# One layer of banded attention and 4-bit dequantized linear: three changes to the order of work on VectorE and POOL

## The chip, the core and the metric

The kernel runs on one core of one Trainium2 chip. A core has TensorE (PE in the profile, with its weight loads as PEld), VectorE (DVE), ScalarE (ACT), GpSimd (POOL) and SyncE (SP, which issues most of the DMAs). Each engine works through its own queue in order; engines wait for each other through semaphores. Matmul results land in PSUM, everything else lives in SBUF. The metric is the device time of one execution in microseconds (us); lower is better.

## The reference

There are 2048 rows of 1024 values, and two stages, each with a residual and a normalization of the rows:

```python
attn = jnp.einsum('ds,td->st', w1, w2) * sparse_mask
y = jnp.einsum('bds,st->bdt', x, attn) + b2
x = _layernorm(x + jax.nn.gelu(y, approximate=False), axis=-1)

e = jnp.linalg.norm(x, axis=-1)
y_l = jnp.einsum('bsi,oi->bso', x, dequant_kbit(qweight, lut4, 4))
y_h = jnp.einsum('bsi,oi->bso', x, dequant_kbit(qweight, lut8, 8))
x = _layernorm(x + jnp.where((e > 64.0)[..., None], y_h, y_l) + bias, axis=-1)
```

`dequant_kbit` builds a 1024 x 1024 weight: bit p of each weight's code comes from bit plane p of `qweight`, and the code picks one of 16 (or 256) values of the output row's table. The mask is banded: it is one only near the diagonal. After the first normalization a row's norm is near 32, so the 8-bit weight is needed only where a row is odd; the kernel counts such rows, and entries of the mask outside the band, and takes a general path if there is any. With these inputs there is none.

## The kernel before

The 2048 rows are 16 tiles of 128 rows. The kernel has four stages, by the time of the profile:

- Up to about 50 us the band of `attn` is made (line 464), with `w2` transposed on TensorE.
- Tiles 0 to 15 go through `attention(n)` (lines 581 to 602). TensorE multiplies the transposed tile with the band on top of b2, which ScalarE copied into the PSUM accumulator before (`fill_b2`, line 505); ScalarE applies gelu (585); VectorE adds the residual and sums the rows (590); `stats` (383) makes the rows' mean on POOL (`nm`, 387), the sum of squares on ScalarE (`junk`, 390) and the factor `r` on POOL (392, 393); and VectorE normalizes the tile in place (`normalize`, 397), for which it needs `r`.
- Meanwhile the 4-bit weight is made in eight blocks of 128 output rows, two blocks (a pair) at a time (`dequantize_pair`, 309). `unpack` (295) spreads the bits of a pair with eight small VectorE instructions. A block has two sides. On each side, ScalarE makes three of the four table entries for bit 0 (`e`, 329) and POOL the fourth (`root`, 333), and VectorE folds them by bits 1 and 2 with three copy_predicated (336 to 338); a last one folds the two sides by bit 3 (346), and the unit matrix is added (349) so that the product carries the residual too. TensorE transposes the block (281) and ScalarE copies it to `wT` (282). The generator is advanced step by step, `steps(1)`, between the tiles, two steps per block. The blocks of a pair are numbered 0 to 7 here; pair 2 is blocks 4 and 5, pair 3 is blocks 6 and 7.
- Tiles 0 to 3 are multiplied with the left half of the weight as soon as blocks 0 to 3 are there (`ffn_half`, 645, "left"), with one attention between each two, and with the right half later; the other twelve tiles go in pairs (`ffn_pair`, 714) from about 200 us to the end. After a left or right product VectorE adds bias (`combine`, 619), which also frees the accumulator.

The order of an engine's queue is not that of the calls. A scheduler of the framework orders the instructions by its own costs and the tiles' buffers; `tc.issue_after(x)` makes every instruction issued inside it, on the engine of `x`, come after `x` in that engine's queue, and holds nothing on other engines. From tile 8 on (`("attention", 8)`, line 876) VectorE's queue is in the order of the calls. The normalization of a tile is not called with its tile: `attention` puts it into a list, and `now()` calls what is in the list, up to tile 8 after the next tile's residual has been called. That is an order of calls alone: the scheduler could put the previous tile's normalization ahead of the next tile's residual, and the unpacks wherever they fit. PSUM has two accumulators `mm` for attentions and half products and four `pt` for transposes.

Of the kernel before, what the change touches and what calls it, by code (L numbers as in the profile page):

```python
# [14 lines left out]
ALU = mybir.AluOpType  # L15
# [6 lines left out]
KT = D // P  # L22
# [170 lines left out]
def kernel(  # L193
# [13 lines left out]
    nc = tc.nc  # L207
# [7 lines left out]
    with ExitStack() as main:  # L215
# [92 lines left out]

        def dequantize_pair(pair):

            bits = bits_of[pair]
            for t in range(2):
                ot = 2 * pair + t

                def plane(p):
                    return bits[:, t * B_L + p, :]

                roots = []
                for side in range(2):
                    root = dq.tile([P, D], FP, tag="root", name="root", bufs=4)  # L320
                    roots.append(root)
                    entry = [root] + [
                        dq.tile([P, D], FP, tag="e", name="e", bufs=7) for _ in range(3)
                    ]
                    for j in (1, 2, 0, 3):
                        k = 4 * side + j
                        d_k, l_k = diff[:, ot, k : k + 1], lt[:, ot, 2 * k : 2 * k + 1]
                        if j:
                            nc.scalar.activation(  # L329
                                entry[j], plane(0), AF.Identity, scale=d_k, bias=l_k  # L330
                            )
                        else:
                            nc.gpsimd.tensor_scalar(  # L333
                                entry[j], plane(0), d_k, l_k, ALU.mult, ALU.add
                            )
                    nc.vector.copy_predicated(entry[2], plane(1), entry[3])  # L336
                    nc.vector.copy_predicated(root, plane(1), entry[1])  # L337
                    nc.vector.copy_predicated(root, plane(2), entry[2])  # L338
                    if side == 0:
                        if t == 1 and pair + 1 < KT // 2:  # L340
                            if pair == 0:
                                tc.keep_in_program_order(differences(2, KT))
                            unpack(pair + 1)
                        yield
                w_nat = roots[0]
                nc.vector.copy_predicated(w_nat, plane(3), roots[1])  # L346

                own = w_nat.rearrange("o (s b) -> o s b", s=8)[:, :, ts(ot, P // 8)]
                nc.vector.tensor_tensor(
                    own, own, ident.rearrange("o (b s) -> o s b", s=8), ALU.add  # L350
                )
                transpose_pending(1)
                pending.append((ot, w_nat))
                yield
# [57 lines left out]
        with tc.tile_pool(name="prod", bufs=1) as prod:  # L412
# [45 lines left out]
            behind = ExitStack()  # L458
# [57 lines left out]
        behind_copy = [None]  # L516
# [57 lines left out]
        def now():  # L574
            while later:
                later.pop(0)()

        def nothing():
            pass

        def attention(n, xT, meanwhile=nothing):
            xt = x_tiles[n]
            ps = band_rows(xT)
# [3 lines left out]
                now()  # L587
            meanwhile()
            total = work.tile([P, 1], FP, tag="total", name="total", bufs=4)
            nc.vector.scalar_tensor_tensor(xt, z, 1.0, xt, ALU.mult, ALU.add, accum_out=total)  # L590
            nm, r, ss = stats(xt, total)

            if n <= 2 * EARLY:
                now()

            def rest():
                normalize(xt, xt, nm, r)
# [277 lines left out]
        for i, (what, n) in enumerate(todo):  # L875
# [27 lines left out]
                    ready = prepare(*todo[i + 1])  # L903
            if (what, n) in unpack_after:

                first = behind_copy[0] if (what, n) == ("left", 0) else masked
                with tc.issue_after(first.ins):
                    steps(1)
        first_ps.close()
        ps_pair = main.enter_context(  # L910
# [54 lines left out]
```

## Time and profile before

Three runs took 357.08, 357.35 and 357.87 us, median 357.35. The profiled execution took 358.36 us, and its span from the first instruction to the last is 356.6 us.

| | busy us | share of the span | instructions |
|---|---|---|---|
| PE | 329.1 | 92% | 1227 |
| DVE | 211.2 | 59% | 310 |
| ACT | 178.7 | 50% | 257 |
| POOL | 114.7 | 32% | 162 |

The mean granted clock of TensorE is 0.978. By stretch, busy us of each engine and the granted clock:

| us | length | PE | DVE | ACT | POOL | PEclk |
|---|---|---|---|---|---|---|
| 57 to 70 | 13 | 12.28 | 11.24 | 8.77 | 10.41 | 1.00 |
| 70 to 82 | 12 | 8.38 | 6.72 | 9.69 | 7.34 | 0.72 |
| 82 to 94 | 12 | 12.00 | 8.71 | 10.52 | 0.00 | 1.00 |
| 94 to 106 | 12 | 12.00 | 10.00 | 11.85 | 5.05 | 1.00 |
| 106 to 118 | 12 | 12.00 | 10.92 | 9.70 | 6.08 | 1.00 |
| 118 to 130 | 12 | 12.00 | 9.95 | 10.70 | 8.51 | 1.00 |
| 130 to 143 | 13 | 9.33 | 8.64 | 9.54 | 2.09 | 0.87 |
| 143 to 156 | 13 | 13.00 | 4.09 | 9.62 | 4.18 | 0.99 |
| 156 to 350 | 194 | 189.92 | 99.91 | 55.22 | 50.61 | 1.00 |

In the lines of the profile, `L560` is line 560 of the kernel, `out<-in` are the program's names without buffer numbers, `x20` is a number of instructions merged into one row, and `[1.24 <-ACT mm L505]` says that the engine was idle for 1.24 us before it, and that ScalarE's instruction of line 505 ended the wait. An engine may wait for several things; the last is named. A POOL instruction's duration holds the time in which it could not reach SBUF.

### The profile page before, as it was taken

How to read it: one execution, taken by the hardware profiler on the slowest of the kernel's cores; microseconds unless marked ns; L12 is line 12 of the kernel's file. 1: busy time of each engine (PE TensorE's matmuls, PEld its weight loads, DVE VectorE, ACT ScalarE, POOL GpSimd, SP SyncE). 2: the span in 40 equal slices, each digit the busy share in tenths (PEclk: the TensorE clock that was granted, in tenths of full speed). 3: DMA queues.
4: the chain of work that ended last, by engine and by line, in shares of the span. 5: the costliest groups of instructions: out<-in, count | busy, mean ns of one | idle time of the engine just before them, and what ended most of it. 6: DMA issues, size and time to landing. Idle time of an engine off the chain costs nothing.

```text
span 356.6 us, 3693 instructions
## 1 busy us (share of the span) xinstructions
PE 329.1 (92%) x1227; PEld 203.3 (57%) x1228; DVE 211.2 (59%) x310; ACT 178.7 (50%) x257; POOL 114.7 (32%) x162
## 2 busy tenths in 40 slices
PE   6799989959999987999999998999999999999990
PEld 6587769845676576966655643444444443444450
DVE  0579898846888885336476853554635525733342
ACT  4696997488997887774346311304214115023020
POOL 1632523870326442324423630502304104004010
PEclk9999999969999998999999999999999999999997
DMA  8999219400000000320264425153554450441103
GB/s 253 317 320 383 90 60 370 160 0 0 1 2 0 0 2 0 149 90 34 72 218 165 140 81 177 59 198 101 202 186 139 181 175 22 192 141 59 59 8 121
DMA packets 28475, 43.91 MB, mean 123 GB/s; under 512 B 7584, under 2 KB 20640, under 8 KB 28448
## 3 DMA queue, kind: packets, MB, share of 16 engines
q1 hardware_dynamic: 26832, 42.66, 34.8%
q10 hardware_dynamic: 1616, 0.93, 0.9%
q8 instruction: 12, 0.20, 0.2%
q14 instruction: 15, 0.12, 0.1%
HBM read 28.90 MB, written 14.68 MB: 122 GB/s over the span
## 4 chain that ended last, share of the span: by engine, by line
PE 60%; DVE 17%; POOL 9%; ACT 5%; issue 4%; DMA 3%; POOLq 0%; DVEq 0%; ACTq 0%
PE u L724 20%; PE mm L607 10%; PE w L724 10%; PE mm L560 8%; PE v L724 6%; POOL root L333 4%; DVE e L336 4%; PE pt L281 3%; DVE root L338 3%; DVE root L346 2%; DMA w_raw<-in_L_attn_w_dram 2%; DVE root L337 2%; POOL nm L387 2%; DVE x L590 2%; PE mm L464 1%
## 5 line engine op out<-in xcount | busy, mean ns | idle before, releaser
L390 ACT ACTIVATE junk<-x,total 128x1024 bf16<-128x1024 f32 x31 | 35.6, 1150 | 64.9 <-DVE total L632 26.2
L560 PE MATMUL mm<-attn,xT 128*128 128x198 f32 (+2 forms) x320 | 62.2, 351 | 5.5 <-ACT mm L505 5.5
L560 PEld LDWEIGHTS mm<-attn,xT 128*128 128x128 f32 x320 | 54.0, 195 | 13.7 <-ACT mm L505 6.9
L329 ACT ACTIVATE e<-v,lt,diff 128x1024 f32<-128x1024 uint8 x48 | 56.9, 1247 | 6.2 <-DVE v L299 3.2
L607 PE MATMUL mm<-wT,xT 128*128 128x512 f32 x128 | 57.8, 605 | 0.0
L333 POOL TENSOR_SCALAR root<-v,diff,lt 128x1024 f32<-128x1024 uint8 x16 | 39.5, 2476 | 44.4 <-DVE root L346 23.2
L387 POOL TENSOR_SCALAR nm<-total 128x1 f32<-128x1 f32 x31 | 19.3, 624 | 77.5 <-DVE x L590 48.9
L724 PE MATMUL u<-t,halves 128*128 128x512 f32 x96 | 43.3, 593 | 1.0 <-DVE x L744 1.0
L607 PEld LDWEIGHTS mm<-wT,xT 128*128 128x128 f32 x128 | 24.4, 196 | 27.8 <-issue 27.3
L710 POOL TENSOR_TENSOR halves<-halves 128x512 f32<-128x512 f32 x6 | 9.5, 1589 | 84.0 <-DVE halves L707 67.8
L706 ACT COPY halves<-rows 128x1024 f32<-128x1024 f32 x6 | 6.3, 1042 | 55.3 <-DMA rows<-there 55.3
L464 PE MATMUL mm<-w2T,w_sb 128*128 128x268 f32 (+1 forms) x128 | 29.2, 377 | 4.2 <-ACT w2T L282 3.6
L724 PEld LDWEIGHTS u<-t,halves 128*128 128x128 f32 x96 | 18.2, 190 | 24.3 <-issue 22.2
L674 DVE STREAM_TRANSPOSE squares<-x 128x1024 f32<-128x1024 f32 x12 | 24.4, 2030 | 11.0 <-DMA there<-squares 11.0
L397 DVE TENSOR_SCALAR x<-x,nm,r 128x1024 f32<-128x1024 f32 x16 | 13.0, 812 | 28.6 <-POOL r L393 24.0
L464 PEld LDWEIGHTS mm<-w2T,w_sb 128*128 128x128 f32 x128 | 22.8, 189 | 8.1 <-ACT w2T L282 4.3
L281 PE MATMUL pt<-ident,x 128*128 128x128 f32 x160 | 22.4, 286 | 3.6 <-ACT wT L282 3.6
L590 DVE SCALAR_TENSOR_TENSOR x<-z,x 128x1024 f32<-128x1024 f32 x16 | 20.5, 1281 | 7.7 <-ACT z L585 7.7
L336 DVE COPY_PREDICATED e<-v,e 128x1024 f32<-128x1024 uint8 x16 | 22.7, 1422 | 3.3 <-ACT e L329 3.3
L281 PEld LDWEIGHTS pt<-ident,x 128*128 128x128 f32 x160 | 19.8, 155 | 6.9 <-ACT wT L282 4.2
L337 DVE COPY_PREDICATED root<-v,e 128x1024 f32<-128x1024 uint8 x16 | 21.0, 1315 | 3.9 <-POOL root L333 3.4
L724 PE MATMUL v<-wT,halves 128*128 128x512 f32 x48 | 22.7, 594 | 0.0
(93 smaller groups left out, 437.6 us busy)
## 6 DMA issues: line engine op xcount, KB each, us to landing
x<-in_L_attn_x_dram SPq DMA_DIRECT2D x16, 512.0 KB, 7.6
out_dram<-o SPq DMA_DIRECT2D x14, 512.0 KB, 2.6
there<-squares SPq DMA_DIRECT2D x12, 512.0 KB, 3.1
rows<-there SPq DMA_DIRECT2D x48, 128.0 KB, 2.9
w_raw<-in_L_attn_w_dram SPq DMA_DIRECT2D x8, 512.0 KB, 6.8
w_sb<-in_L_attn_w_dram SPq DMA_DIRECT2D x3, 1024.0 KB, 7.8
w_sb<-in_L_attn_w_dram SPq DMA_DIRECT2D x2, 512.0 KB, 7.1
x<-_L_attn_sparse_mask_dram SPq DMA_DIRECT2D x2, 413.0 KB, 3.7
```

The costliest lines, as they stand in the source:

```text
L281: nc.tensor.transpose(pt[:, j, :], block(g * (HALF // P) + j), ident)
L329: nc.scalar.activation(entry[j], plane(0), AF.Identity, scale=d_k, bias=l_k)
L333: nc.gpsimd.tensor_scalar(entry[j], plane(0), d_k, l_k, ALU.mult, ALU.add)
L336: nc.vector.copy_predicated(entry[2], plane(1), entry[3])
L337: nc.vector.copy_predicated(root, plane(1), entry[1])
L387: nc.gpsimd.tensor_scalar(nm, total, -1.0 / D, None, ALU.mult)
L390: nc.scalar.activation(junk, u, AF.Square, scale=float(-D), bias=total, accum_out=ss)
L464: part = nc.tensor.matmul(out=ps[:, : hi - lo], lhsT=w1_sb[s][:, k, :], rhs=w2T[:, k, lo:hi], start=(k == 0), stop=(k == KT - 1),)
L560: behind_mm[0] = nc.tensor.matmul(out=ps[:, a:b], lhsT=xT[:, s, :], rhs=attn[:, s, a - lo : b - lo], start=False, stop=hi == D or (h == 0 ...
L590: nc.vector.scalar_tensor_tensor(xt, z, 1.0, xt, ALU.mult, ALU.add, accum_out=total)
L607: nc.tensor.matmul(out=ps, lhsT=xT[:, k, :], rhs=wT[:, k, ts(h, HALF)], start=(k == 0), stop=(k == KT - 1),)
L724: nc.tensor.matmul(out=ps, lhsT=a[:, k, :], rhs=b[:, k, :], start=start and k == 0, stop=stop and k == KH - 1, skip_group_check=True,)
```

## The change

Three edits.

1. In `attention`, for tiles 0 to 8, the previous tile's normalization is put behind this tile's residual in VectorE's queue, by `issue_after`; it was only called after it.
2. The bits of pair 2 (blocks 4 and 5) are unpacked in the generator's first step of pair 2 itself, and no longer in the third step of pair 1. That step is the one taken after `("left", 0)`; in it, VectorE's instructions now come after the last mask multiplication and after the latest residual called, that of tile 3, and ScalarE's after the copies of the early tile, as before. (Before, in that step, nothing on VectorE was held.)
3. In blocks 4 to 7, the entry `j == 2` of the second side is made on POOL and not on ScalarE: four instructions.

In the built programs the queues of TensorE and SP are unchanged. VectorE's queue has the same instructions: the residuals of tiles 1, 2 and 3 come earlier, the normalizations of tiles 0 to 2 each come after the next tile's residual (that of tile 3 is called by the left product of tile 0 and is not bound), and all 16 unpacks of pairs 2 and 3 follow tile 3's residual, five ahead of tile 3's normalization and eleven behind it. Further on, the copies of blocks 4 to 7 stand in another order around the combines; the last block's are all ahead of the combine of tile 3's left half, where four instructions of block 7 came after it. In POOL's queue the entries of block 4 and 5 now stand behind the statistics of tiles 1 to 3, five entries in a row, and later entries stand in part between a tile's sum and its factor. ScalarE's queue has four entries less.

```diff
         def dequantize_pair(pair):
 
+            if pair == 2:
+                unpack(pair)
             bits = bits_of[pair]
...
-                        if j:
+                        if j and not (ot > 3 and side and j == 2):
                             nc.scalar.activation(
                                 entry[j], plane(0), AF.Identity, scale=d_k, bias=l_k
                             )
                         else:
                             nc.gpsimd.tensor_scalar(
                                 entry[j], plane(0), d_k, l_k, ALU.mult, ALU.add
                             )
...
-                        if t == 1 and pair + 1 < KT // 2:
+                        if t == 1 and pair + 1 < KT // 2 and pair != 1:
...
+        behind_sum = [None]
...
-            nc.vector.scalar_tensor_tensor(xt, z, 1.0, xt, ALU.mult, ALU.add, accum_out=total)
+            summed = behind_sum[0] = nc.vector.scalar_tensor_tensor(
+                xt, z, 1.0, xt, ALU.mult, ALU.add, accum_out=total
+            )
             nm, r, ss = stats(xt, total)
 
             if n <= 2 * EARLY:
-                now()
+                with tc.issue_after(summed.ins):
+                    now()
...
-                first = behind_copy[0] if (what, n) == ("left", 0) else masked
-                with tc.issue_after(first.ins):
+                with ExitStack() as behind:
+                    behind.enter_context(tc.issue_after(masked.ins))
+                    if (what, n) == ("left", 0):
+                        behind.enter_context(tc.issue_after(behind_copy[0].ins))
+                        behind.enter_context(tc.issue_after(behind_sum[0].ins))
                     steps(1)
```

## The prediction

> **What bounds the kernel now.** I read the page's slices first, then who made TensorE wait, then the order of time of each engine between 57 and 156 us. The slices say where TensorE is not full:
>
> ```profile
> PE   6799989959999987999999998999999999999990
> PEclk9999999969999998999999999999999999999997
> ```
>
> One slice is 8.9 us. After the start there are two dips, at 71 to 80 us and at 134 to 143 us, and in both the granted clock (PEclk) dips too. From 155.76 us to the last matmul TensorE waits only 0.37 and 1.00 us, so what reaches 155.76 earlier ends earlier. The waits of TensorE, in all us, times, longest:
>
> ```profile
> PE mm L560 <- ACT mm L505: 5.5, 4, 2.4
> PE pt L281 <- ACT wT L282: 3.6, 2, 2.8
> ```
>
> TensorE in order of time (start, us, line, idle before and releaser):
>
> ```profile
> 69.64 1.91 PE L281 MATMUL pt<-ident,root 128*128 128x128 f32 x16
> 74.39 2.51 PE L281 MATMUL pt<-ident,x 128*128 128x128 f32 x12 [2.84 <-ACT wT L282]
> 77.67 1.11 PE L281 MATMUL pt<-ident,x 128*128 128x128 f32 x4 [0.77 <-ACT wT L282]
> 78.58 8.59 PE L607 MATMUL mm<-wT,xT 128*128 128x512 f32 x16
> ...
> 132.40 3.86 PE L560 MATMUL mm<-attn,xT 128*128 128x198 f32 x20 [1.24 <-ACT mm L505]
> 136.10 1.04 PE L281 MATMUL pt<-ident,x 128*128 128x128 f32 x8
> 139.56 5.54 PE L560 MATMUL mm<-attn,xT 128*128 128x198 f32 x20 [2.43 <-ACT mm L505]
> ```
>
> The product at 78.58 took 8.59 us, the later ones 7.03; the attention at 139.56 took 5.54, others 3.76. So each dip costs its wait and 1.6 to 1.8 us of half clock. ScalarE is the one named, but it was itself held in its queue, by VectorE:
>
> ```profile
> 71.71 1.15 ACT L390 ACTIVATE junk<-x,total 128x1024 bf16<-128x1024 f32 x1 [4.88 <-DVE x L590]
> ...
> 131.33 1.02 ACT L505 COPY mm<-b_bc 128x1024 f32<-128x1024 f32 x1 [1.45 <-DVE x L619]
> ```
>
> And VectorE in order of time, with its largest wait between 76 and 140 us below:
>
> ```profile
> 70.46 1.21 DVE L590 SCALAR_TENSOR_TENSOR x<-z,x 128x1024 f32<-128x1024 f32 x1
> ...
> 110.86 2.04 DVE L338 COPY_PREDICATED root<-v,e 128x1024 f32<-128x1024 uint8 x1
> ...
> 130.62 0.67 DVE L619 SCALAR_TENSOR_TENSOR x<-mm,bias_bc 128x512 f32<-128x512 f32 x1
> ```
>
> ```profile
> DVE x L397 <- POOL r L393: 7.5, 4, 3.5
> ```
>
> ```profile
> 108.30 3.40 POOL L333 TENSOR_SCALAR root<-v,diff,lt 128x1024 f32<-128x1024 uint8 x1 [8.05 <-DVE root L346]
> ```
>
> The residual of tile 2 (L590 at 70.46) had its gelu at 66.84; it stood behind a normalization (L397) that waited 1.02 us for POOL's r, and behind unpacks. From 80.74 (first copy_predicated of block 4) to 135.56 VectorE is the slow one: 28 copies, and TensorE at 132 and 139 waits for what comes after them. POOL's entry at 108.30 waited for VectorE until 110.82, then ran, and VectorE's next copy took 2.04 us instead of 1.31: the two exclude each other.
>
> **The change part by part.** Lines are those of before.
>
> *Edits 1 and 2, normalizations behind the next residual, block 4 and 5 unpacked behind tile 3's residual.* Nothing is added or removed; 16 unpacks (0.20 us each) and four normalizations (0.81) change place on VectorE, and POOL's first entries of block 4 move behind the statistics of tiles 1 to 3. TensorE's order, SP's order and all DMAs stay. Attention of tile 2 ends on TensorE at 61.46 + 3.76 = 65.2; gelu 1.02, so the residual starts near 66.3 instead of 70.46. ScalarE's square (1.25) then ends at 68.8, tile 3's gelu at 69.8, its residual at 71.0, its square at 72.4 (three wT copies run before it), the fourth wT copy at 72.9, four transposes 0.45: the first product starts near 73.3 instead of 78.58, 5.3 us earlier. TensorE's idle there is in pieces under 2 us, so I let it run at full clock: another 1.6 us. VectorE after residual 3 (71.0): a normalization 0.73, five unpacks 1.0, the normalization of tile 3 once r is there (square's end + 1.1 = 73.5) to 74.2, eleven unpacks to 76.4, then the wait for POOL's first entry, about 0.95 after VectorE lets go (97.42 to 98.42 in the trace was 1.0): first copy at 77.4 instead of 80.74. This is 3.3 us, and only this is worth anything later, since TensorE's lead of 7 us runs into VectorE's dequantization.
>
> *Edit 3, four entries from ScalarE to POOL.* ScalarE loses 4 x 1.15 = 4.6 us; that only frees VectorE's waits for it, 0.93 and 0.76. POOL gains four entries. An entry took 1.20 us with VectorE idle, 4.42 at most, 2.47 on average between 45 and 145 us. Three costs, none of them shown by before:
> - Five entries stand in a row on POOL (four roots and one of the new ones) from about 74.8; VectorE asks for the fifth near 83.7 (77.4, four copies, a combine and one exclusion). At 1.20 each it waits nothing, at 2.47 each 3.5 us; I take 2.0, since the last ones run while VectorE is idle.
> - POOL's queue has a new entry between tile 4's sum and its power, so r, for which VectorE waited 1.96 us there, comes later by 1.20 (VectorE is then idle, so the lone price); ends 0 and 4.42.
> - Exclusion: 2.04 against 1.31 is 0.73 per entry on VectorE's path; four give 0 to 2.9, I take one, 0.7.
>
> What is queued behind these waits is the combine of the left half (L619), which frees TensorE's accumulator.
>
> **The sum.** Combine of tile 3 on VectorE: before at 130.62, 49.9 us after the first copy. In the new order the last four dequantization operations of block 7 (131.22 to 135.56, 4.3 us) stand ahead of it. Removed: the waits 0.93, 0.76 and, as the product is earlier, the 1.55 us for TensorE at 87.20; 3.2. Added: 2.0 + 1.2 + 0.7 = 3.9. So 77.4 + 49.9 + 4.3 - 3.2 + 3.9 = 132.3. From it follow the b2 copy (+0.71), gelu of tile 7 (+0.95, then 1.02) and its residual, at 135.0 instead of 135.56: TensorE's attention moves from 139.56 to 139.1, -0.5. But the attention before it now waits for the same combine: it starts near 134.1 instead of 132.40 and ends, with transposes, at 138.7, so the idle before 139.1 is 0.4 instead of 2.43 us, and the clock should hold: 5.54 becomes 3.76, -1.8. Against it +0.5, since ScalarE's copy at 150.10 was hidden by the slow attention and now is not. Sum: -0.5 - 1.8 + 0.5 = **-1.8 us** at 155.76, and so at the end. The x loads of the last tiles (4.6 us to landing) follow the release of the dequantization's memory and move with it; they cost nothing, and would cost up to 1 us if they did not. The profiled execution took 358.36 (span 356.6), 1.0 above the median of 357.35; I take the difference off the median: **355.5 us**.
>
> **The rivals.**
>
> *POOL gets in sooner (352.8).* If POOL is granted at the end of whatever VectorE runs, the 2.0 and 0.7 go: 355.5 - 2.7 = 352.8. For it: at 44.64 a copy that had been issued 0.10 before the end of the last one took 2.13, and an unpack at 69.41 took 1.13, so POOL got in between two that stood close. Against it: the entry at 61.40 (4.41 us) let two such boundaries pass. The Trainium skill, "SBUF — State Buffer", section "Who interferes with whom", says that whoever issues first gets the shared ports for the whole instruction and the other blocks fully, which speaks for a grant at each instruction's end; the rows at 61.40 and 108.30 say that VectorE's next instruction is mostly there first. By that rule the time would be this rival's.
>
> *POOL becomes the bound (359.3), slower.* If the new entries on blocks 5 to 7 each stand ahead of a tile's r and take 4.4 us instead of 2.5, one such hold at the end, +1.9, moves the combine to 134.2, tile 7's residual to 136.9, after 135.56; TensorE idles over 2 us again and the half clock returns, +1.8: -1.8 + 1.9 + 1.8 = +1.9. It decides once more than 1.8 us are added to the 3.9. For it: 7.5 us of VectorE's waits already end on POOL's r. Against it: VectorE's waits are idle time in which POOL runs at 1.20.
>
> *The gain is given back (356.9).* The opening's 3.3 us are spent before 130 and the half clock at 139 stays, with the copy at 150.10 hidden as before: -0.5. For it: idles of 2.84 and 2.43 us halved the clock, 1.24 did not, so 1.5 to 2 us is open. The Trainium skill, "TensorE: Matmul & The Clock Gate", section "What's actually happening", has the clock judged over free-running windows of 3413 ns, so the same idle may or may not halve it; the trace agrees in that idles shorter than a window did.
>
> **How the numbers follow.** Forecast 0.49 (its own range 354.3 to 356.6), POOL sooner 0.20, POOL the bound 0.17, given back 0.14. This kernel tells 0.2% (0.7 us) from no change. Faster 0.49 + 0.20 = 0.69, same 0.14, slower 0.17. The range goes from the faster rival with 0.4 below it, 352.4, to 358.4: the 0.17 of the slower rival is mostly left out, but a smaller form of it, +1.0, is in. If all three costs sat at their upper ends (3.5, 4.42, 2.9: 6.9 more) the time would be 362; at the lower ends, 351.6.
>
> **What would show it.** Right: residual of tile 2 near 66, the first product near 73 at 6.9 to 7.0 us; the slice at 71 to 80 back to 9 in PEclk; VectorE's first copy of block 4 near 77; VectorE waiting 1 to 4 us for POOL's entries, which now appear as a releaser with e as output; the combine of tile 3 after the last copy_predicated, near 132; no half clock at 139. Wrong: TensorE idle over 2 us at several left products between 95 and 130 (VectorE's combine behind a normalization that waits for r), or the last copy_predicated later than 133.

## The result and the profile after

The changed kernel took **356.16 us**, the median of 20 runs (355.52 to 356.92), against 357.01 us for the kernel before in 20 runs beside them (355.79 to 359.19). The ratio is 0.997, with a 95% interval of 0.9957 to 0.9983: 0.85 us, or 0.3%, faster. The forecast was 355.5 us with a range of 352.4 to 358.4.

Times of the kernel before fall into two groups, near 356.9 and near 358.6 us (spans near 355.1 and 356.8), and the profiled execution on which the prediction worked, with 358.36 us, is one of the upper group; the changed kernel shows one group.

The profiled execution of the changed kernel took 356.57 us, its span is 354.8. The slices of the page of after (a slice is 8.9 us here):

```profile
PE   7799989989969888999999998999999999999990
PEclk9989999999999899999999999999999999999996
```

The dip of the granted clock at 71 to 80 us is gone, and so is that at 134 to 143, where PE shows 8 and not 7. New is a stretch at 98 to 133 us in which PE shows 6, 9, 8, 8 (slices 12 to 15), with the clock down once. The waits of TensorE between 45 and 160 us name who is behind it (in all us, times, longest):

```profile
PE mm L614 <- DVE x L626: 4.6, 2, 2.8
PE mm L562 <- ACT mm L507: 3.7, 5, 1.2
```

Before, TensorE never waited there for VectorE's combine (now line 626). The same in order of time (start, us, then the idle time before and its releaser):

```profile
73.50 7.13 PE L614 MATMUL mm<-wT,xT 128*128 128x512 f32 x16
...
100.98 7.10 PE L614 MATMUL mm<-wT,xT 128*128 128x512 f32 x16 [2.77 <-DVE x L626]
...
116.66 8.72 PE L614 MATMUL mm<-wT,xT 128*128 128x512 f32 x16 [1.81 <-DVE x L626]
...
138.78 3.86 PE L562 MATMUL mm<-attn,xT 128*128 128x198 f32 x20 [0.21 <-ACT mm L507]
```

The first left product starts 5.08 us earlier than before (73.50 against 78.58) and runs at full clock. The third and the fourth wait for a combine, and the fourth runs 8.72 us, with the granted clock halved for 3.41 us from 116.48 on. The attention that took 5.54 us at 139.56 takes 3.86 at 138.78. VectorE of after, in order of time:

```profile
66.33 1.23 DVE L594 SCALAR_TENSOR_TENSOR x<-z,x 128x1024 f32<-128x1024 f32 x1 [2.40 <-ACT z L589]
...
74.36 4.00 DVE L299 TENSOR_SCALAR v<-q 128x256 int32<-128x256 int32 x11
78.27 1.30 DVE L339 COPY_PREDICATED root<-v,e 128x1024 f32<-128x1024 uint8 x1
...
86.10 1.32 DVE L338 COPY_PREDICATED e<-v,e 128x1024 f32<-128x1024 uint8 x1 [1.07 <-POOL e L335]
...
99.42 0.81 DVE L399 TENSOR_SCALAR x<-x,nm,r 128x1024 f32<-128x1024 f32 x1 [3.35 <-POOL r L395]
100.15 0.68 DVE L626 SCALAR_TENSOR_TENSOR x<-mm,bias_bc 128x512 f32<-128x512 f32 x1
```

and, in a later stretch, the combine of tile 3:

```profile
132.03 0.69 DVE L626 SCALAR_TENSOR_TENSOR x<-mm,bias_bc 128x512 f32<-128x512 f32 x1
```

The wait of 3.35 us at 99.42 is for `r`, and POOL's order of time shows a new entry (output `e`) between the two halves of `r`:

```profile
97.37 0.19 POOL L394 TENSOR_SCALAR r<-ss 128x1 f32<-128x1 f32 x1
97.66 1.20 POOL L335 TENSOR_SCALAR e<-v,diff,lt 128x1024 f32<-128x1024 uint8 x1
98.81 0.57 POOL L395 TENSOR_TENSOR r<-r,minus_half 128x1 f32<-128x1 f32 x1
```

The combine at 100.15, which frees the accumulator for the product at 100.98, stands in VectorE's queue behind the normalization that waits for this `r`.

### The profile page after: what moved, and what is told of

The parts are those of the page before. It is cut to its first block, busy times and chain, and to the rows that moved or that the text cites. A ratio compares the mean times of both kernels' runs of the same rounds, so it can differ in the third digit from the quotient of the medians.

```text
span 354.8 us, 3694 instructions
## 1 busy us (share of the span) xinstructions
PE 328.8 (93%) x1228; PEld 202.6 (57%) x1228; DVE 212.6 (60%) x310; ACT 174.5 (49%) x253; POOL 126.9 (36%) x166
## 4 chain that ended last, share of the span: by engine, by line
PE 56%; DVE 13%; POOL 11%; ACT 9%; DMA 4%; issue 4%; SPq 2%; POOLq 0%; DVEq 0%; ACTq 0%
PE u L731 21%; PE w L731 10%; PE mm L562 8%; PE mm L614 8%; PE v L731 6%; POOL root L335 4%; DVE e L338 3%; ACT e L331 3%; POOL nm L389 2%; DVE root L340 2%; PE pt L281 2%; DMA w_sb<-in_L_attn_w_dram 2%; ACT junk L392 2%; DVE root L348 2%; DMA q<-in_L_ffn_qweight_dram 1%
## 5 line engine op out<-in xcount | busy, mean ns | idle before, releaser
L562 PE MATMUL mm<-attn,xT 128*128 128x198 f32 (+2 forms) x320 | 60.5, 345 | 3.7 <-ACT mm L507 3.7
L562 PEld LDWEIGHTS mm<-attn,xT 128*128 128x128 f32 x320 | 52.7, 191 | 11.6 <-ACT mm L507 5.1
L331 ACT ACTIVATE e<-v,lt,diff 128x1024 f32<-128x1024 uint8 x44 | 52.0, 1240 | 2.8 <-issue 1.4
L335 POOL TENSOR_SCALAR root<-v,diff,lt 128x1024 f32<-128x1024 uint8 x16 | 37.6, 2354 | 38.4 <-DVE v L299 21.8
L389 POOL TENSOR_SCALAR nm<-total 128x1 f32<-128x1 f32 x31 | 23.0, 743 | 68.6 <-DVE x L594 39.7
L713 ACT COPY halves<-rows 128x1024 f32<-128x1024 f32 x6 | 6.2, 1042 | 54.9 <-DMA rows<-there 54.9
L466 PE MATMUL mm<-w2T,w_sb 128*128 128x268 f32 (+1 forms) x128 | 30.2, 386 | 1.2 <-DVE attn L488 0.5
L594 DVE SCALAR_TENSOR_TENSOR x<-z,x 128x1024 f32<-128x1024 f32 x16 | 21.3, 1334 | 12.0 <-ACT z L589 12.0
L338 DVE COPY_PREDICATED e<-v,e 128x1024 f32<-128x1024 uint8 x16 | 24.2, 1514 | 2.6 <-ACT e L331 1.5
L281 PE MATMUL pt<-ident,x 128*128 128x128 f32 x160 | 21.2, 276 | 1.2 <-ACT wT L282 0.9
L731 PE MATMUL w<-wT,halves 128*128 128x512 f32 x48 | 21.7, 594 | 0.4 <-DVE x L748 0.4
```

What stands on the lines that cost most here:

```text
L281: nc.tensor.transpose(pt[:, j, :], block(g * (HALF // P) + j), ident)
L331: nc.scalar.activation(entry[j], plane(0), AF.Identity, scale=d_k, bias=l_k)
L335: nc.gpsimd.tensor_scalar(entry[j], plane(0), d_k, l_k, ALU.mult, ALU.add)
L389: nc.gpsimd.tensor_scalar(nm, total, -1.0 / D, None, ALU.mult)
L466: part = nc.tensor.matmul(out=ps[:, : hi - lo], lhsT=w1_sb[s][:, k, :], rhs=w2T[:, k, lo:hi], start=(k == 0), stop=(k == KT - 1),)
L562: behind_mm[0] = nc.tensor.matmul(out=ps[:, a:b], lhsT=xT[:, s, :], rhs=attn[:, s, a - lo : b - lo], start=False, stop=hi == D or (h == 0 ...
```

## The experiments

Three theories stood after the result: that the POOL entries give back what the opening gained; that ScalarE's relief by the entries is the gain; and that VectorE can't use a lead of TensorE at all. All ratios below are to the kernel before, run beside each group of experiments on the same chip. The table has how the profiled executions come through the stage (start of the four left products, then of the first right product, us). In the "warm" rows TensorE repeats transposes in the idle stretches of before, the first ahead of 74.39 us, the second ahead of 139.56. A start has a scatter of its own: in the five kernels that have both edits 1 and 2, and so nearly the same opening, the first left product starts between 72.69 and 73.51 us.

| | 1st | 2nd | 3rd | 4th | right | span | median of the runs | ratio (95%) |
|---|---|---|---|---|---|---|---|---|
| before | 78.58 | 92.35 | 104.58 | 117.67 | 155.76 | 356.6 | 357.01 | 1 |
| after | 73.50 | 85.83 | 100.98 | 116.66 | 153.97 | 354.8 | 356.16 | 0.997 (0.9957 to 0.9983) |
| edits 1 and 2 | 72.93 | 85.25 | 98.11 | 111.74 | 149.50 | 350.3 | 352.69 | 0.9872 (0.985 to 0.9894) |
| edit 1 | 75.41 | 87.73 | 99.95 | 113.05 | 151.41 | 352.2 | 353.90 | 0.9899 (0.9878 to 0.992) |
| edit 2 | 73.90 | 86.21 | 98.44 | 112.09 | 150.69 | 351.9 | 353.28 | 0.9877 (0.9854 to 0.99) |
| edit 3 | 78.13 | 90.46 | 102.67 | 117.91 | 155.15 | 356.0 | 357.83 | 1.0026 (1.0006 to 1.0047) |
| after, entries left out | 73.39 | 85.71 | 98.37 | 114.00 | 151.62 | 352.4 | 354.01 | 0.9908 (0.9881 to 0.9934) |
| after, combine first | 72.69 | 85.02 | 98.10 | 112.43 | 150.20 | 351.0 | 354.50 | 0.9921 (0.9894 to 0.9948) |
| edits 1 and 2, combine first | 73.51 | 85.83 | 98.06 | 111.19 | 148.17 | 349.0 | 350.68 | 0.9816 (0.9779 to 0.9853) |
| before, both places warm | 79.65 | 92.57 | 104.79 | 117.89 | 152.70 | 353.6 | 355.27 | 0.9952 (0.9931 to 0.9973) |
| before, second place warm | 78.62 | 92.77 | 104.98 | 118.09 | 154.80 | 355.6 | 356.23 | 0.9964 (0.994 to 0.9988) |
| before, first place warm | 78.25 | 90.57 | 102.79 | 115.89 | 152.28 | 353.1 | 355.48 | 0.9948 (0.9928 to 0.9969) |

### Edits 1 and 2 without the POOL entries

The changed kernel with the old condition for ScalarE:

```diff
-                        if j and not (ot > 3 and side and j == 2):
+                        if j:
```

> The first two edits without the four new POOL entries. Theory (POOL's entries give the gain back): the opening is as in the changed kernel, first left product near 73.5 us instead of 78.58, and the waits that the entries made go: of the 3.35 us that VectorE waited for r at 99.42 about 1.4 (it was 1.96 before the change), the 1.07 us for the entry at 86.10, and most of TensorE's 2.77 and 1.81 us for a combine. So 4 to 5 us under the kernel before, near 352.5. Rival 1 (ScalarE's relief is the gain): without it no gain, 356.5 to 357.5. Rival 2 (VectorE can't use the lead, whatever POOL does): as the changed kernel, 0.5 to 1.5 us under the kernel before.

Measured: 352.69 us, ratio 0.9872 (0.985 to 0.9894), 4.3 us faster than before. The first two edits alone are worth five times what the whole change is worth, and VectorE does use the lead. Its waits between 76 and 140 us in this kernel (in all us, times, longest):

```profile
DVE x L399 <- POOL r L395: 6.3, 4, 2.2
DVE x L594 <- ACT z L589: 3.7, 1, 3.7
DVE root L339 <- POOL root L335: 0.9, 1, 0.9
```

There is no row with `ACT e` in it. The two waits for ScalarE's entries of 0.93 and 0.76 us, of which the prediction had edit 3 relieve VectorE, have gone without edit 3. So has a third one, which before had for the first left product:

```profile
87.20 0.69 DVE L619 SCALAR_TENSOR_TENSOR x<-mm,bias_bc 128x512 f32<-128x512 f32 x1 [1.55 <-PE mm L607]
```

The first copy of block 4 and the combine of tile 3 in the kernel with edits 1 and 2:

```profile
77.71 1.32 DVE L339 COPY_PREDICATED root<-v,e 128x1024 f32<-128x1024 uint8 x1
...
125.31 0.71 DVE L626 SCALAR_TENSOR_TENSOR x<-mm,bias_bc 128x512 f32<-128x512 f32 x1
```

Four instructions of block 7 stand behind that combine, as before, and no left product waits for a combine; the third waits 0.47 us, by the profile for a ScalarE entry.

### The POOL entries alone

The third edit on the kernel before:

```diff
-                        if j:
+                        if j and not (ot > 3 and side and j == 2):
```

> The four entries moved to POOL alone, on the kernel before. Theory: slower by 1.5 to 3.5 us (each entry 1.2 to 2.5 us on POOL ahead of a tile's r, for which VectorE already waited 7.5 us; ScalarE's 4.6 us were not what TensorE waited for). Rival 1 (ScalarE's relief is the gain): faster by 0.5 to 1.5 us. Rival 2: within 0.7 us of the kernel before.

Measured: 357.83 us, ratio 1.0026 (1.0006 to 1.0047): 0.9 us slower, less than the expectation's price. On top of edits 1 and 2 the same edit costs 3.5 us (4.3 less 0.85). Its fourth left product starts at 117.91, no earlier than before (117.67), although the third, with the first at full clock, was 1.91 us ahead. A part of the price comes back at the end of the stage: as in the changed kernel, the attention near 139 now waits 0.21 instead of 2.43 us and takes 3.86 instead of 5.54. The profile with edits 1 and 2 has no half clock there that could be won back.

This run shows something else that mattered later. TensorE, in order of time:

```profile
74.36 1.64 PE L281 MATMUL pt<-ident,x 128*128 128x128 f32 x12 [2.88 <-ACT wT L282]
...
78.13 7.13 PE L607 MATMUL mm<-wT,xT 128*128 128x512 f32 x16
```

It is the idle time of before (2.88 against 2.84 us) at the same place (74.36 against 74.39), and yet the product behind it runs at full clock, 7.13 against 8.59 us.

### Each of the first two edits alone

The normalizations bound behind the next residual, nothing else:

```diff
-                now()
+                with tc.issue_after(summed.ins):
+                    now()
```

> The first edit alone: each normalization of tiles 0 to 2 behind the next tile's residual, unpacks and entries where they were. Theory: the residual of tile 2 no longer stands behind a normalization that waits 1.02 us for r, so most of the 5 us of the opening come from this edit, and the time is 3 to 5 us under the kernel before. If the unpacks of block 4 to 7 are what held the residual, it is 0 to 1.5 us under it.

And the unpacking behind tile 3's residual, nothing else:

```diff
+            if pair == 2:
+                unpack(pair)
...
-                        if t == 1 and pair + 1 < KT // 2:
+                        if t == 1 and pair + 1 < KT // 2 and pair != 1:
...
+                    if (what, n) == ("left", 0):
+                        behind.enter_context(tc.issue_after(behind_copy[0].ins))
+                        behind.enter_context(tc.issue_after(behind_sum[0].ins))
```

> The second edit alone: the bits of blocks 4 and 5 unpacked behind tile 3's residual, normalizations free. Theory: with the unpacks gone from the opening POOL's first entries of block 4 also go from it, and the statistics no longer stand behind them; 2 to 5 us under the kernel before. If the normalization is the only thing that held the residual, within 1 us of the kernel before. Both this and the edit before it at 3 us or more would say that each alone clears the opening.

Measured: 353.90 us (0.9899, 0.9878 to 0.992) and 353.28 us (0.9877, 0.9854 to 0.99). Each takes 3.1 and 3.7 us off, both together 4.3. By the expectation, both at 3 us or more says that each alone clears most of the opening. They don't add, since both remove work that VectorE does ahead of the residuals of tiles 1 to 3: tile 3's residual starts at 74.65 before, at 71.89 with edit 1, at 70.39 with edit 2 and at 69.36 with both. In the profile of edit 2 alone the attention that stood at 139.56 is this row:

```profile
134.56 5.48 PE L562 MATMUL mm<-attn,xT 128*128 128x198 f32 x20 [2.42 <-ACT mm L507]
```

and in the profile of the two edits together the same attention, after the same idle time, is this:

```profile
134.30 3.86 PE L562 MATMUL mm<-attn,xT 128*128 128x198 f32 x20 [2.44 <-ACT mm L507]
```

An idle of 2.4 us halves the clock in one execution and not in another; the last section shows what tells the two apart.

### TensorE kept warm in the kernel before

Transposes of block 3 are made four times over and those of tile 10's x three times, so that TensorE works in the two idle stretches of before; the output is unchanged:

```diff
+        again = [1]
...
-                for j in range(HALF // P):
+                for j in list(range(HALF // P)) * again[0]:
...
+                again[0] = 4 if ot == 3 else 1
...
+            again[0] = 3 if n == SOON - 2 else 1
```

> The kernel before, with the transposes of weight block 3 made four times and those of tile 10's x made three times, so that TensorE has work in the two idle stretches ahead of which its clock was halved (records of 6.83 us at 74.88 and 3.41 us at 139.73). Output unchanged. Theory A (the change gained -1.8 trace against trace and only -0.85 by the medians because the kernel before spends a changing time at half clock, most of it at these two places): the half clock at both places goes, the times lie closer together than before's 2 to 3 us, and the median comes 1.5 to 3 us under before's (half of 6.83 + 3.41 is 5.1 us of TensorE's work, and VectorE and ScalarE hide a part of it). Rival B (the time lies in the wait for the transposed weight and for the normalization, not in the clock): within 0.7 us of before, with the same spread. Rival C (the repeated transposes themselves lie on the path): 1 us or more slower.

Measured: 355.27 us, ratio 0.9952 (0.9931 to 0.9973), 1.8 us faster than before with TensorE given more to do; 10 of the 12 times lie between 354.94 and 355.66. Theory A's size and its narrower spread came. Its profile does not show the gain at the first place: a half clock of 3.41 us, instead of 6.83, is still there from 77.63 on, behind an idle of 2.07 us; the last transposes run at it, the first left product starts at 79.65, and the fourth at 117.89, no earlier than before. What this execution gains, it gains behind that, up to the right product (table).

### The entries left out

The changed kernel, in which the four entries are computed by no engine (the expectation says which part of the weight is thereby left out):

```diff
-                        if j and not (ot > 3 and side and j == 2):
+                        if ot > 3 and side and j == 2:
+                            entry[2] = entry[1]
+                        elif j:
```

> The changed kernel with the four entries that went to POOL not computed at all, by any engine: entry 2 of side 1 of blocks 4 to 7 is taken from entry 1 (this part of the dequantization is left out). Theory A (edit 3 costs 3.5 us on top of the other two through POOL's time: its lock between VectorE's operations, and r behind a new entry): 351.0 to 353.0, no idle of 1.8 us or more ahead of a left product for a combine, and no half clock at 116; at 352.7 the relief of ScalarE is worth nothing, at 351 it is worth VectorE's 0.9 + 0.8 us of waits for ScalarE. Rival B (ScalarE was needed where it was: what costs is the order of the work that the change leaves on ScalarE and VectorE, not POOL): 355 to 356.5, with the idle of 2.8 and 1.8 us still ahead of the left products.

Measured: 354.01 us, ratio 0.9908 (0.9881 to 0.9934). It falls between the ranges of the two theories. Without any work for these entries the kernel is 2.2 us faster than the changed one (3.0 off before against 0.85), so that much goes with the entries' work on POOL (a bound, as VectorE's order differs from the changed kernel's in a few places too). But it is 1.3 us slower by the medians than the kernel that makes all four on ScalarE, and 2.1 by the spans of the profiles. So no gain of relieving ScalarE is left to see, and a part of edit 3's price remains when the work is gone: the order. VectorE in this kernel:

```profile
88.41 1.30 DVE L340 COPY_PREDICATED e<-v,e 128x1024 f32<-128x1024 uint8 x1
89.59 1.22 DVE L596 SCALAR_TENSOR_TENSOR x<-z,x 128x1024 f32<-128x1024 f32 x1
...
95.60 0.81 DVE L401 TENSOR_SCALAR x<-x,nm,r 128x1024 f32<-128x1024 f32 x1 [2.04 <-POOL r L397]
```

The scheduler puts an `e` copy ahead of tile 4's residual, here and in the changed kernel (residual at 90.88). In the kernel with edits 1 and 2 it stands behind that residual, which runs at 87.95. (Lines of this kernel are two further down, L340 is L338 of after.) TensorE's fourth product pays:

```profile
114.00 7.13 PE L616 MATMUL mm<-wT,xT 128*128 128x512 f32 x16 [2.28 <-DVE x L628]
```

The wait for `r` is 2.04 us here and 3.35 in the changed kernel. The difference, 1.31, is but for 0.1 the entry of 1.20 us that stood ahead of the power.

### The combine ahead of the normalization

In the changed kernel, and in the one with edits 1 and 2, the left half's combine is issued ahead of the deferred normalization:

```diff
-            now()
-            combine(n, h, ps[:, :HALF], bias_bc[:, ts(h, HALF)])
+            if h:
+                now()
+            combined = combine(n, h, ps[:, :HALF], bias_bc[:, ts(h, HALF)])
+            with tc.issue_after(combined.ins):
+                now()
```

> The changed kernel with the combine of a left half ahead of the deferred normalization in VectorE's order (in the changed kernel VectorE waited 3.35 us for POOL's r at 99.42, and the combine at 100.15 that frees the accumulator stood behind that; TensorE's product at 100.98 had waited 2.77 us, and the next one 1.81). Theory A (the price of the POOL entries is paid through the accumulator: the combine stands behind a wait for POOL): the waits of 2.8 and 1.8 us for a combine go, with them the half clock at 116.48, and the time falls by 3 to 5 us to 351 to 353. Rival B (VectorE's own queue is the bound from 78 on, and its wait for r costs the same wherever the combine stands): VectorE only puts one combine of 0.7 us into each wait, 354.8 to 356.2.

> The first two edits without the POOL entries, with the combine of a left half ahead of the deferred normalization. In the run of the two edits VectorE waited 6.3 us in four waits for POOL's r between 76 and 140, 2.23 of it at 94.12, and TensorE waited 0.5 us for no combine. Theory A (without the POOL entries the accumulator is free in time, and what bounds is VectorE's queue): the combines fill 0.7 us of up to four waits, 350 to 352.7. Rival B (r is the bound and anything put ahead of the normalization makes the tile's transposes late): 353 to 355. Both say that it stays under the kernel before and the changed one.

The edit acts on all four left products; at the first it also puts the normalization of tile 3 behind the combine of tile 0, so that the sixteen unpacks run in a row ahead of it.

Measured: 354.50 us on the changed kernel, ratio 0.9921 (0.9894 to 0.9948), with a spread of 352.79 to 356.33, and **350.68 us** on the two edits, ratio 0.9816 (0.9779 to 0.9853). For the first, the median lies just under theory B's range, and the profiled execution (352.79 us, the fastest of its runs) within theory A's. In that execution the mechanism is the one that A named. TensorE in the changed kernel with the combine first:

```profile
98.10 7.10 PE L614 MATMUL mm<-wT,xT 128*128 128x512 f32 x16 [0.68 <-DVE x L626]
...
129.32 5.54 PE L562 MATMUL mm<-attn,xT 128*128 128x198 f32 x20 [3.54 <-ACT mm L507]
```

The idle of 2.77 us is 0.68, that of 1.81 is 0.42, and the fourth left product, at 112.43, has no half clock any more (7.13 us). What was saved collects in front of the attention at 129.32, which now waits 3.54 us and pays the half clock. The order of an instruction of 0.7 us was worth about 1.7 us of the median (2.55 off before against 0.85); what spreads this kernel's times was not traced.

For the second, VectorE's order of time shows the two instructions changed round:

```profile
95.74 0.67 DVE L626 SCALAR_TENSOR_TENSOR x<-mm,bias_bc 128x512 f32<-128x512 f32 x1
96.54 0.81 DVE L399 TENSOR_SCALAR x<-x,nm,r 128x1024 f32<-128x1024 f32 x1
```

Without the swap VectorE waited 2.23 us at 94.12 for `r`; here it copies and combines meanwhile, and the normalization finds `r` ready. Rival B, that what is put ahead makes tiles late, is refuted. This is the best version found: 6.4 us (1.8%) under before, and well under the changed kernel. Its profile still has 3.04 us of idle and a half clock, at the attention at 131.98.

### Which half clock spreads the times

The kernel before was profiled again, unchanged:

> The kernel before, unchanged, for a second profiled execution. Its times fall into two groups, spans near 355.0 and near 356.8, and the one on the page is of the second (356.6). Theory A (the groups differ by whether the clock is halved at 139.73 for 3.41 us, which made the attention there take 5.54 us rather than 3.76): an execution of the first group, span 354.9 to 355.3, shows no record there, the attention near 139.5 takes 3.76 to 3.9, and the right half's first product starts near 154.0 instead of 155.76; the record of 6.83 us at 74.88 stays. Rival B (the groups differ elsewhere, at the opening or behind 160): the attention near 139.5 takes 5.5 in both. An execution of the second group tells nothing.

It came out in the upper group (358.53 us), and its rows are those of the prediction:

```profile
78.41 8.62 PE L607 MATMUL mm<-wT,xT 128*128 128x512 f32 x16
...
139.74 5.47 PE L560 MATMUL mm<-attn,xT 128*128 128x198 f32 x20 [2.43 <-ACT mm L505]
```

So this run decides nothing between its theories. The two repetitions of transposes one at a time, the second place first (`again[0]` is 3 for tile 10's x alone):

> The kernel before with the transposes of tile 10's x alone made three times, in the idle stretch of 2.43 us ahead of the attention at 139.56. Theory A (this half clock of 3.41 us comes in a part of the executions and makes before's second group): no time of the group near 358.6 is left, the times lie within about 1 us, and the median is that of before's first group, 356.6 to 357.0. Rival B (the idle stretch costs, the clock doesn't): both groups stay. Rival C (the half clock is in every execution): the median falls by 1.5 to 2 us, to about 355.3.

Measured: 356.23 us, ratio 0.9964 (0.994 to 0.9988), still with two groups, near 355.7 and near 357.2 (before beside it: 356.8 and 358.8). None of the three expectations holds as a whole. Both groups moved, by 1.1 and 1.6 us: work in the second place is worth that much in either (nearest to rival C, though smaller than it said), and the half clock at 139.7 does not make the groups. VectorE's and POOL's queues are in the order of before here. Its profile, of the upper group:

```profile
78.62 8.94 PE L613 MATMUL mm<-wT,xT 128*128 128x512 f32 x16
...
139.96 3.86 PE L566 MATMUL mm<-attn,xT 128*128 128x198 f32 x20 [0.67 <-ACT mm L509]
```

Then the first place alone (`again[0]` is 4 for block 3 alone):

> The kernel before with the transposes of weight block 3 alone made four times, in the idle stretch of 2.84 us ahead of the first left product. The run with both places kept warm was 1.8 us under before. Theory A (the 6.83 us at half clock at 74.88 are in every execution and are worth 1.5 us, 8.59 against 7.13 for the first left product): 355.0 to 355.8, with a second group 1.8 us above it. Rival B (TensorE's lead there is worth nothing, since VectorE's dequantization stands behind it, and the 1.8 us were all from the second place): 356.5 to 357.1.

Measured: 355.48 us, ratio 0.9948 (0.9928 to 0.9969), all 12 times between 354.89 and 355.99. The size is theory A's; its second group did not come. But the run does not decide between A and rival B, which is the prediction's own view of TensorE's lead, since it touched more than the clock of the first left product. With the longer transposes the scheduler ordered VectorE, POOL and ScalarE anew, as in the run with both places warm. A copy of the next side now stands ahead of the combine of tile 0, and one more copy of block 7 ahead of that of tile 3:

```profile
85.65 1.32 DVE L339 COPY_PREDICATED root<-v,e 128x1024 f32<-128x1024 uint8 x1
86.85 0.68 DVE L625 SCALAR_TENSOR_TENSOR x<-mm,bias_bc 128x512 f32<-128x512 f32 x1
```

In this profile the second place has healed as well: the idle times there are 2.12 and 1.08 us instead of 1.24 and 2.43, and no half clock follows:

```profile
78.25 7.13 PE L613 MATMUL mm<-wT,xT 128*128 128x512 f32 x16
...
131.26 3.86 PE L566 MATMUL mm<-attn,xT 128*128 128x198 f32 x20 [2.12 <-ACT mm L509]
...
137.09 3.86 PE L566 MATMUL mm<-attn,xT 128*128 128x198 f32 x20 [1.08 <-ACT mm L509]
```

Up to the fourth left product this execution is 1.78 us ahead of before (115.89 against 117.67), at the right product 3.48. So a part of the 1.7 us can come from the second place by the new order, where the run before this one found 1.1 to 1.6, and how much the first place is worth alone stays open.

Last, the kernel before a third time, in search of its lower group:

> The kernel before, unchanged, for a profiled execution of its first group (span near 355.0). Measured so far: with the first place alone kept warm no second group is left (353.1 to 354.2), with the second place alone kept warm both groups stay and both come 1.1 to 1.5 us earlier. Theory A (the groups differ by how long the clock is halved in the first left product; the half clock at 139.7 is in both): in an execution of the first group the first left product takes 7.0 to 7.5 us instead of 8.59, the record at 74.9 is missing or half as long, and the attention near 138 still takes about 5.5. Rival B (the groups differ at 139.7): the first left product takes 8.6 and the attention near 139.5 3.8. An execution of the second group tells nothing.

It took 359.1 us, the upper group again: the first left product 8.90 us, the attention at 140.30 5.54. What the experiments show is that the groups are gone in the two kernels with the first place kept warm and stay when only the second is; as the first two also have the new order of VectorE, it is not shown that the clock of the first product makes the groups. That the lower group runs the first product at full clock, or nearer to it, fits this; but no execution of that group was traced.

## Why the prediction was right, and where it was not

**The opening (edits 1 and 2): right in its rows.** Tile 2's residual was put near 66.3 and came at 66.33; the first left product was put near 73.3 at full clock and came at 73.50, 7.13 us. The first copy of block 4 was put at 77.4 and came at 78.27, 0.87 late. The step that failed there is "eleven unpacks to 76.4": at 0.20 us each they were to take 2.2 us, and they took 4.00. POOL's first entry starts at 75.23, among them, and the excess of 1.8 us lies beside it; in the run without the new entries the eleven took 4.00 as well, so it isn't edit 3's. The 0.95 us of waiting for POOL behind them did not come.

**"Only this is worth anything later, since TensorE's lead of 7 us runs into VectorE's dequantization": wrong.** It was argued from VectorE being the slow one between 80 and 135, and the prediction's own sum contradicts it, by taking off the 1.55 us for TensorE at 87.20. In the kernel with edits 1 and 2 the first copy is 3.0 us earlier (77.71 against 80.74) and the combine of tile 3 5.3 us (125.31 against 130.62), since VectorE's waits for ScalarE's entries (0.93, 0.76) and for TensorE (1.55) vanish too; the first right product starts 6.3 us earlier.

**Edit 3's gain: credited wrongly.** "That only frees VectorE's waits for it, 0.93 and 0.76": edits 1 and 2 remove these waits by themselves, and with the entries left out altogether the kernel isn't faster than with them on ScalarE. On the kernel before, edit 3 alone does leave 0.40 and nothing of them, and is slower all the same. No run shows a gain in time from the relief of ScalarE.

**Edit 3's price: right as a total, in one of its three terms.** The wait for the fifth entry was taken as 2.0 and was 1.07; `r` behind a new entry was taken as 1.2 and is 1.31 (3.35 against 2.04). The exclusion of 0.7 can't be separated in any run. What the sum booked as the new order, 4.3 us for block 7's last four operations ahead of the combine, is an effect of edit 3 also: with edits 1 and 2 alone they stand behind it. By the prediction's own terms edit 3 put the combine of tile 3 later by 3.9 + 4.3 - 0.93 - 0.76 = 6.5 us, and the two profiles differ by 132.03 - 125.31 = 6.7, of which 0.56 is there at the first copy already. By the same terms edits 1 and 2 alone put it earlier by 3.3 + 1.55 = 4.9 us; measured, 5.3. So the working held a gain of some 5 us at this place and a loss of over 6, and the text never took them apart; apart, they would have priced edit 3 as a loss. That the sum of 132.3 came within 0.3 of the measured 132.03 is also luck: the first copy came 0.87 late, and the stretch from it to the combine took 53.76 us instead of 54.9, of which 0.93 is the wait for the fifth entry.

**The end of the stage: right.** The attention was put at 139.1 behind an idle of 0.4 us and at full clock; it is at 138.78, behind 0.21, 3.86 us. The +0.5 for ScalarE's copy is the 0.42 us ahead of the attention at 149.40. The sum of -1.8 us at the first right product is met by the two profiled executions, 155.76 to 153.97, -1.8, and their spans, 356.6 to 354.8, -1.8. Behind it TensorE waits three times and not, as the prediction read it, twice; the third wait, of 0.88 us, is in both profiles (at 296.12 and 294.33) and changes nothing.

**What was named as a sign of error and came in part.** TensorE idled 2.77 and 1.81 us at two left products (over 2 us at several was the sign), since the combine stood behind a normalization that waited for POOL's `r`, and the clock was halved at 116.48. Of the lead of 6.5 us at the second product 1.0 was left at the fourth (table). It did not upset the sum, because this went over VectorE's combine, which had the delay in it. The run with the combine first shows that a part of it was avoidable: about 1.7 us.

**"I take the difference off the median": the term that was mis-sized.** The medians differ by 0.85 us, not by 1.8. The profiled execution of before was 1.35 us above the median of 20 runs, that of after 0.41; the difference, 0.94, is what is missing. The text saw the profile 1.0 us above the three runs shown and let it pass. The half clock of the first product, 1.6 us in the sum for the opening, is a price that the profiled execution paid; that executions of the lower group pay less of it would fit, but none was traced. The forecast came out 0.66 too low and not 0.94, since the three runs shown had a median 0.34 above that of the 20.

**The rivals.** *POOL becomes the bound* did not come, though the price of POOL was real. *POOL gets in sooner* is half true: five entries in a row took 10.8 us (75.23 to 86.06), 2.17 each, between the 1.20 of a free one and the 2.47 of before. A grant at each instruction's end, which this rival needs, is not what the rows show: the mean of tile 4, a POOL instruction of 3.93 us at 92.19, let the ends of three VectorE instructions pass (93.36, 94.57 and 94.84). *The gain is given back* has a part of the truth in the medians, but not at its place: no half clock is left at 139. The Trainium skill, "TensorE: Matmul & The Clock Gate", section "What's actually happening", says that the clock is judged over free-running windows of 3413 ns; the traces agree (between 57 and 160 us the records at half clock are 3413 and 6827 ns long, and they lie differently in each execution).

## What to carry to other kernels

Price each part of a change on its own, at one place in the trace, before adding up: here a gain of 4.3 us and a loss of 3.5 stood behind a result of 0.85, and the loss was the part that relieved an engine for which nobody waited any more. When instructions move between engines, look in the built order for what moved around them, above all an instruction that frees a buffer and now stands behind a wait: putting a combine of 0.7 us ahead of a normalization gave 1.7 us in one kernel and 2 in another. The same goes for an experiment: repeating transposes on TensorE alone changed the order of three other queues, and so could not price the clock. And a profiled execution that lies above the median carries a cost that typical runs may not pay; a half clock after 2 to 3 us of idle is the first suspect.

## What the hardware showed beyond expectation

- The same idle halves the clock in one execution and not in the next: 2.84 and 2.86 us did in three profiles of the kernel before, 2.88 did not in the run of edit 3 alone; 2.42 and 2.43 did, 2.44 did not. What tells them apart is where the idle lies. The changes of the clock in one execution lie on a grid of 3.413 us, and the grid lies differently in each execution. Between 57 and 160 us the fourteen traces have 14 halvings. In each the grid interval that ends where the half clock begins holds 1.89 to 3.39 us of idle TensorE; the other intervals at full clock hold at most 1.77, but for one with 1.98 (entries left out, from 110.28 on). The idle of 2.42 us at 134.56 with edit 2 alone lies with 2.32 in one interval; that of 2.44 at 134.30 with edits 1 and 2 is cut at 133.61, and 1.75 is the larger part; the 2.88 with edit 3 alone is cut at 72.61, and the larger part is 1.75.
- A kernel in which TensorE does useless work in its idle time was faster: by 1.7 us with the first place (0.9948, 0.9928 to 0.9969), with 1.1 us between the extremes of its times instead of 3.4. How much of it is the clock, and how much the new order of the other queues, is open.
- A POOL instruction of a single column is held up by VectorE as a whole entry is: the mean of tile 4 (line 389, 128x1) took 3.93 us at 92.19 in after while VectorE worked without a gap, and the same instruction of a later tile 0.22 at 136.09, with VectorE idle.

```profile
92.19 3.93 POOL L389 TENSOR_SCALAR nm<-total 128x1 f32<-128x1 f32 x1 [6.12 <-DVE x L594]
...
136.09 0.22 POOL L389 TENSOR_SCALAR nm<-total 128x1 f32<-128x1 f32 x1 [6.95 <-DVE x L594]
```
